# A Mamba and attention hybrid in float32: the residual added by TensorE in the turn to tokens, the last product with C by halves, z projected later in the period, and half tiles two apart

## The chip, the core and the metric

The kernel runs on one core of a Trainium2 chip. The metric is the device time of one launch in microseconds. The engines are named as in the profile: PE is TensorE (matrix multiplications; PEld its weight loads), DVE is VectorE, ACT is ScalarE, POOL is GpSimd, and SP is SyncE, which here issues most of the DMAs. Each engine works through its own queue in program order, and waits at an instruction whose inputs or whose buffer are not ready.

## What is computed

The input x has 8 batches of 128 channels and 64 x 64 pixels, so 4096 positions in each batch. There are two layers.

The first is a Mamba block over the positions, with a group norm and a residual:

```python
xz = x @ W_in;  xh, z = split(xz)                # 256 channels each
xh = silu(causal_conv_k2(xh)); x_dbl = xh @ W_x  # dt_low, B, C
dt = softplus(dt_low @ W_dt + b_dt)
h = exp(dt * A) * h + dt * B * xh;  y = sum_n h * C   # scan over positions, 16 states
y = (y + xh * D) * silu(z);  out = y @ W_out
x = silu(group_norm(out)) + x                    # the residual
```

The second layer turns x into tokens t and adds a causal additive attention (scores from tanh of a sum of two projections, summed over 16 units; weights exp(scores) below the diagonal), and then a mixture of 64 experts with the top 8 tokens for each expert. The kernel computes the sums of tanh as ratios of exponentials, D (denominators) and N (numerators), each a matrix product of vectors U and V.

## The kernel before, in words

The launch has a fast path and a general path behind a flag; only the fast path runs here. It has three stages.

**Mamba** (function `mamba`, L255 to L588). The positions are cut into 64 chunks of 512 (8 for each batch). A written-out loop, L530 to L588, runs "periods". In each period every chunk in flight is taken one step further: chunk c1 is projected, c2 gets its step sizes, c3 is scanned, c4 is gated and projected back, c5 is normalised, c6 gets its residual and c7 is turned to tokens in the same period, c8 is layer-normed, c9 gets the vectors U and V, c10 is saved to DRAM. From c5 on a chunk lies a batch (8 chunks) behind, since the group norm needs the whole batch. The order of the calls in the loop is the order of each engine's queue. 64 chunks and the lag make 79 periods: the first ones have no late steps, the last ones no early ones.

Only three of the 16 states are scanned (NR = 3); the others are summed by `over` and `others`, and `vanish` collects a number that shows whether that is allowed. Steps that matter here, with their lines:

- `project` (L283), `gate` (L294) and `silus` (L302 to L304): the projections of x and z on PE, then silu on ACT.
- `rows` (L311 to L324): B, C and the low-rank step; ACT copies bc (L315), GpSimd writes it to DRAM (L317), SP reads it back over all partitions as rep (L319), DVE forms prod (L324), which frees the PSUM buffer that the second `steps` matmul needs.
- `steps` (L330), `magnitudes` (L340 to L343), `logarithm` (L347), `rounded` (L351) and `inputs` (L356 to L360): softplus, spread over ACT and DVE.
- `decays` (L383, ACT, into two PSUM buffers of tag da), `drive` (L387, DVE), `scan` (L396, DVE) and `outputs` (L402, GpSimd: state times C), three times each, one for each state.
- `others` (L369, DVE), which reads the PSUM tile of `over` (L364, PE).
- `sums` (L408 and L410 on PE, L412 on DVE): the states' products are added by matmuls with the identity. `gated` (L416), `back` (L421), `store` (L430 on ACT, L431 on DVE).
- `normal` (L444, ACT), `residual` (L448, GpSimd), `turn` (L455, PE transposes; L457, ACT's copy to tt).
- `moments` (L461 to L471), `tokens` (L478), `turn_back` (L487 to L490), `vectors` (L498 to L502), `save` (L505).

PSUM is shared by tags: "s" has two buffers in turn (for pbc, both pdt, both py, pt, pb and po), and "pz" has one, for over, pz and puv. On SBUF, "db" is a ring of three (three drives and w in each period), tt and uv have one buffer each.

**Attention** (function `attend`, from L591). A tile is one block of 128 keys (jb) against 512 queries (ic). Above the diagonal blocks of a row a tile is narrower. The list `tiles` has for each row ic its full tiles, then a tile of two pieces (384 and 128 columns, so 512 in all), and last a half tile of 256 columns. There are 136 tiles for each batch, 1088 in all. Round i of the main loop (L1066 to L1090) works on several tiles at once:

```python
rounds(cur, nxt)        # PE: N of tile i and D of tile i + 2
inverses(i, nxt, last)  # ACT: ln of D (L650, L651), exp (L653, or L656 and L659)
causal(i - 2); ratios(cur); scores(cur)   # DVE L664, L665, L673, L678; GpSimd L666
weigh(i - 3)            # PE: weights times tokens (L687), into av
```

D and N of one round are three matrix products each, on row groups of 32, 32 and 64 rows of the array (L631). `weigh` starts the sum av at the tile with jb = 0, and ends it at the half tile, after which DVE copies it (L696). Between these steps the round takes a few items of the lanes `finishing` and `routing`, which hold the work at the end of a row and the choice of the experts' tokens. `bring` (L741 to L746) loads U, V, tt and tok of a chunk by SP, U and V in six pieces each.

**Experts** (from L1091): loads of weights, the small products, and the result.

## Time and profile before

| | |
|---|---|
| three runs, median (lowest to highest) | 6251.23 us (6249.23 to 6251.68) |
| profiled execution, its own time | 6249.68 us |
| its span, from first to last instruction | 6248.0 us |
| mean granted PE clock | 0.955 |
| busy PE, DVE, ACT, POOL | 93%, 78%, 80%, 32% of the span |
| DMA | 426.65 MB, 68 GB/s in the mean |

A row of the timeline has its start in us from the span's start, its length in us, the engine, the line, the operation with output<-inputs, the count where neighbours are merged, and in brackets the idle time of the engine before it and what released it. A row of a group has the count, then busy us and mean ns of one, then idle us before it. The granted clock is a share of full speed. Durations of matmuls are modelled and overlap; their starts give the pitch.

### The profile page before, as it was taken

The page shows a single profiled execution, that of the slowest core. Times are in us where ns is not written, and L with a number is a line of the kernel's source. Part 1 is how long each engine was busy: PE and PEld are TensorE (multiplying, and loading weights), DVE is VectorE, ACT ScalarE, POOL GpSimd, SP SyncE. Part 2 cuts the span into 40 slices and gives each one's busy share as a digit, 9 for nine tenths or more (in the row PEclk, how much of TensorE's full clock was granted, in tenths as well). Part 3 has the DMA queues.
Part 4 walks back from the last instruction along what each step waited for, and adds up shares of the span by engine and source line. Part 5 has one row for each costly group of instructions (what it writes and reads, how often), then busy time and mean ns, then how long its engine had stood idle before and what let it go on. Part 6 is the DMA issues. An engine that isn't in the chain of part 4 may idle for free. (4 is left out here: it accounts for less than half of the span.)

```text
span 6248.0 us, 69479 instructions
## 1 busy us (share of the span) xinstructions
PE 5802.7 (93%) x22714; PEld 2254.2 (36%) x22714; DVE 4860.9 (78%) x7829; ACT 4986.9 (80%) x5657; POOL 1992.1 (32%) x1652
## 2 busy tenths in 40 slices
PE   7888888888869999999999999999999999999987
PEld 2333333333323334333333333433333333343335
DVE  7999999999937777777777777777777777777741
ACT  5677777777658998898899889889889988988941
POOL 2333333333313332333333233233333323323311
PEclk8999999999879999999999999999999999999988
DMA  2234333333340011010101101101010110110058
GB/s 82 75 123 132 128 132 132 132 126 128 115 150 26 24 33 34 24 44 27 31 13 46 33 24 33 34 24 44 26 33 13 46 33 24 33 35 24 15 206 294
DMA packets 182406, 426.65 MB, mean 68 GB/s; under 512 B 32578, under 2 KB 33234, under 8 KB 171282
## 3 DMA queue, kind: packets, MB, share of 16 engines
q1 hardware_dynamic: 172514, 403.48, 19.9%
q0 software_dynamic: 9376, 18.37, 0.8%
q8 instruction: 182, 2.98, 0.2%
q14 instruction: 190, 1.56, 0.1%
q10 hardware_dynamic: 144, 0.26, 0.0%
HBM read 295.12 MB, written 126.88 MB: 68 GB/s over the span
## 5 line engine op out<-in xcount | busy, mean ns | idle before, releaser
L631 PE MATMUL D<-U,V 32*128 32x512 f32 (+7 forms) x6912 | 2730.8, 607 | 16.6 <-DMA U<-uv_dram 13.3
L631 PE MATMUL N<-U,V 32*128 32x512 f32 (+7 forms) x6912 | 2366.0, 608 | 46.6 <-DVE mix L664 44.3
L666 POOL TENSOR_TENSOR mix<-mix 128x512 f32<-128x512 f32 (+1 forms) x1088 | 1348.1, 1239 | 2833.7 <-DVE mix L664 2713.5
L653 ACT ACTIVATE mix<-mix 128x2048 f32<-128x2048 f32 x973 | 1853.2, 1905 | 31.0
L678 DVE TENSOR_TENSOR mix<-mix,mix 128x512 f32<-128x512 f32 (+1 forms) x1088 | 736.4, 677 | 920.1 <-POOL mix L666 919.9
L650 ACT ACTIVATE mix<-D 128x1024 f32<-128x1024 f32 (+1 forms) x1088 | 1077.3, 990 | 442.1 <-PE N L631 398.7
L631 PEld LDWEIGHTS D<-U,V 32*128 32x128 f32 (+1 forms) x6912 | 886.2, 185 | 1425.6 <-issue 533.8
L664 DVE TENSOR_TENSOR mix<-mix,N 128x1024 f32<-128x1024 f32 (+1 forms) x1088 | 1284.9, 1181 | 31.6 <-PE N L631 24.6
L687 PE MATMUL av<-mix,tok 128*128 128x512 f32 (+3 forms) x2304 | 1209.0, 611 | 30.0 <-DVE sums L696 28.8
L631 PEld LDWEIGHTS N<-U,V 32*128 32x128 f32 (+1 forms) x6912 | 710.8, 185 | 267.1 <-DVE mix L664 230.4
L665 DVE TENSOR_TENSOR mix<-mix,N 128x512 f32<-128x512 f32 (+1 forms) x1088 | 722.6, 664 | 1.8 <-PE N L631 1.8
L651 ACT ACTIVATE mix<-D 128x512 f32<-128x512 f32 (+1 forms) x1088 | 632.4, 581 | 17.7 <-PE N L631 15.3
L687 PEld LDWEIGHTS av<-mix,tok 128*128 128x128 f32 x2304 | 350.5, 189 | 802.2 <-issue 692.6
L402 POOL TENSOR_TENSOR hc<-hs,rep 128x1024 f32<-128x1024 f32 x192 | 453.0, 2369 | 472.3 <-issue 369.6
L396 DVE TENSOR_TENSOR_SCAN hs<-da,hs,db 128x512 f32<-128x512 f32 x336 | 412.3, 1269 | 10.8 <-ACT da L383 4.1
L410 PE MATMUL py<-hc,ident 128*128 128x512 f32 x768 | 354.1, 597 | 0.0
L383 ACT ACTIVATE da<-dt,aneg 128x512 f32<-128x512 f32 x384 | 259.2, 688 | 62.8 <-DVE hs L396 50.7
L283 PE MATMUL px<-xt,wtap 128*128 128x512 f32 x512 | 288.2, 692 | 3.9 <-DMA xt<-in_x_dram 3.9
L317 POOL DMA_DIRECT2D bc_dram<-bc x128 | 68.8, 542 | 520.5 <-ACT bc L315 520.3
L387 DVE TENSOR_TENSOR db<-dx,rep 128x1024 f32<-128x1024 f32 x192 | 228.0, 1215 | 0.1
L410 PEld LDWEIGHTS py<-hc,ident 128*128 128x128 f32 x768 | 149.7, 195 | 193.7 <-issue 193.4
L487 PE MATMUL pb<-ident,tok 128*128 128x128 f32 x256 | 74.3, 386 | 153.4 <-DVE tok L478 153.4
(243 smaller groups left out, 5659.0 us busy)
## 6 DMA issues: line engine op xcount, KB each, us to landing
rep<-bc_dram SPq DMA_DIRECT2D x64, 1536.0 KB, 7.0
uv_dram<-uv SPq DMA_DIRECT2D x64, 768.0 KB, 3.5
xr<-in_x_dram SPq DMA_DIRECT2D x64, 256.0 KB, 3.3
k_dram<-tt SPq DMA_DIRECT2D x64, 256.0 KB, 7.3
k_dram<-tok SPq DMA_DIRECT2D x64, 256.0 KB, 7.5
U<-uv_dram SPq DMA_DIRECT2D x128, 128.0 KB, 2.9
V<-uv_dram SPq DMA_DIRECT2D x128, 128.0 KB, 2.9
U<-uv_dram SPq DMA_DIRECT2D x256, 64.0 KB, 2.0
```

The costliest lines, as they stand in the source:

```text
L396: nc.vector.tensor_tensor_scan(hs[:, h, :], ch[c].pop(("da", n, h)), db[:, h, :], first, ALU.mult, ALU.add)
L402: nc.gpsimd.tensor_tensor(hc, ch[c]["hs", n], ch[c]["rep"][:, 1, n, :].unsqueeze(1).to_broadcast([P, 2, CH]), ALU.mult)
L410: nc.tensor.matmul(py, lhsT=ident, rhs=ch[c]["hc", n][:, h, :], start=False, stop=n == NR - 1)
L631: nc.tensor.matmul(t12[:, g - 1, at : at + n] if g else t0[:, at : at + n], lhsT=V[b, jb // NQ][r, ab, ts(jb % NQ, P)], rhs=U[b, ic][r, ab ...
L650: nc.scalar.activation(x[:, 1:3, lo:], d12[:, :, lo:], AF.Ln)
L651: nc.scalar.activation(x[:, 0, lo:], d0[:, lo:], AF.Ln)
L653: nc.scalar.activation(x[:, :, lo:], x[:, :, lo:], AF.Exp, scale=-1.0)
L664: nc.vector.tensor_tensor(r[:, 1:3, lo:], r[:, 1:3, lo:], n12[:, :, lo:], ALU.mult)
L665: nc.vector.tensor_tensor(r[:, 0, lo:], r[:, 0, lo:], n0[:, lo:], ALU.mult)
L666: nc.gpsimd.tensor_tensor(mix[k + 1][:, 3, lo:], r[:, 1, lo:], r[:, 2, lo:], ALU.add)
L678: nc.vector.tensor_tensor(s, s, mix[k - 2][:, 0, lo:], ALU.add)
L687: nc.tensor.matmul(av[0][:, q : q + n], lhsT=tok[b, jb // NQ][:, jb % NQ, :], rhs=mix[k + 1][:, 3, at : at + n], start=first, stop=last,)
```

## The change

In the Mamba periods the GpSimd addition of the residual is gone. `turn` adds it on PE instead: for each of four blocks a matmul of o with the identity and one of xr with the identity go into the same PSUM block. The copy to tt is a step of its own (`taken`), at the place where `turn` was; `turn` itself comes earlier, right after `gated`. The last of the three products with C is issued as two halves. `others` moves from before the scans to after the sums. `silus` is split: x first, then `gate`'s z, whose silu comes after `normal`. The tile of `vanish` is taken from the ring db, tt has two buffers, and the uv of every other chunk of the last batch takes a buffer of rep.

In attention the half tile comes first in the odd rows, and before the tile of two pieces in the even rows, so that the half tiles of two neighbouring rows stand two places apart in the list; the tile of two pieces now ends the row. `weigh` takes the first two tiles of an odd row in exchanged order, both in one round, and none in the next. `bring` loads the rows of the small groups first, and for the first chunk of all it issues U by ACT and V by GpSimd.

```diff
@@ -295,11 +295,13 @@
                     pz[:, h, :], lhsT=wgate[:, ts(h, P)], rhs=ch[c]["x"][:, 1:], start=True, stop=True
                 )
-        def silus(c):
+        def silu_x(c):
             xc = ch[c]["xc"] = pair("xc", f"xc{c}", 4)
             px = ch[c].pop("px")
             for h in range(2):
                 nc.scalar.activation(xc[:, h, :], px[:, h, :], AF.Silu, bias=convb[:, h : h + 1])
+        def silu_z(c):
             zs = ch[c]["zs"] = pair("zs", f"zs{c}", 4)
             nc.scalar.activation(zs, ch[c].pop("pz"), AF.Silu)
@@ -371,10 +373,10 @@
             )
         def vanish(c):
+            z = pair("db", f"fade{c}", 3)
             for h in range(2):
-                z = mw.tile([P, CH], F32, tag="fade", bufs=1, name=f"fade{c}_{h}")
                 nc.scalar.activation(
-                    z, ch[c]["dt"][:, h, :], AF.Exp, scale=fade[:, h : h + 1], accum_out=faded[:, c, h : h + 1]
+                    z[:, h, :], ch[c]["dt"][:, h, :], AF.Exp, scale=fade[:, h : h + 1], accum_out=faded[:, c, h : h + 1]
                 )
         def decays(c, n):
@@ -399,9 +401,12 @@
         def outputs(c, n):
             hc = ch[c]["hc", n] = pair("hc", f"hc{c}_{n}", 5)
-            nc.gpsimd.tensor_tensor(
-                hc, ch[c]["hs", n], ch[c]["rep"][:, 1, n, :].unsqueeze(1).to_broadcast([P, 2, CH]), ALU.mult
-            )
+            for h in ((slice(0, 2),) if n < NR - 1 else (slice(0, 1), slice(1, 2))):
+                hs = ch[c]["hs", n][:, h, :]
+                nc.gpsimd.tensor_tensor(
+                    hc[:, h, :], hs, ch[c]["rep"][:, 1, n, :].unsqueeze(1).to_broadcast(list(hs.shape)), ALU.mult
+                )
         def sums(c, h):
             py = single(f"py{c}_{h}")
@@ -443,18 +448,18 @@
             b, o = c // NCH, ch[c]["o"]
             nc.scalar.activation(o, o, AF.Silu, bias=norm[:, b, 1:2], scale=norm[:, b, 0:1])
-        def residual(c):
-            o = ch[c]["o"]
-            nc.gpsimd.tensor_tensor(o, o, ch[c].pop("xr"), ALU.add)
         def turn(c):
-            o = ch[c].pop("o")
+            o, xr = ch[c].pop("o"), ch[c].pop("xr")
             pt = single(f"pt{c}").rearrange("p (q c) -> p q c", c=P)
             for q in range(NQ):
-                nc.tensor.transpose(pt[:, q, :], o[:, ts(q, P)], ident)
-            t = ch[c]["t"] = mw.tile([P, NQ, P], F32, tag="tt", bufs=1, name=f"tt{c}")
-            nc.scalar.copy(t, pt)
+                nc.tensor.matmul(pt[:, q, :], lhsT=o[:, ts(q, P)], rhs=ident, start=True, stop=False)
+                nc.tensor.matmul(pt[:, q, :], lhsT=xr[:, ts(q, P)], rhs=ident, start=False, stop=True)
+            ch[c]["pt"] = pt
+        def taken(c):
+            t = ch[c]["t"] = mw.tile([P, NQ, P], F32, tag="tt", bufs=2, name=f"tt{c}")
+            nc.scalar.copy(t, ch[c].pop("pt"))
         def moments(c):
             t = ch[c]["t"]
@@ -496,7 +501,12 @@
             puv = psum.tile([P, 2, CH], F32, tag="pz", name=f"puv{c}")
             for s in range(2):
                 nc.tensor.matmul(puv[:, s, :], lhsT=wuv[:, s, :], rhs=xT, start=True, stop=True)
-            uv = ch[c]["uv"] = mw.tile([P, 3, CH], F32, tag="uv", bufs=1, name=f"uv{c}")
+            if c < NC - NCH or c % 2:
+                uv = mw.tile([P, 3, CH], F32, tag="uv", bufs=1, name=f"uv{c}")
+            else:
+                uv = mw.tile([P, 2, NR, CH], F32, tag="rep", bufs=2, name=f"uv{c}")[:, 0]
+            ch[c]["uv"] = uv
             nc.scalar.activation(uv[:, 0, :], puv[:, 0, :], AF.Exp, bias=shift)
             nc.scalar.activation(uv[:, 1, :], puv[:, 1, :], AF.Exp, bias=biasv)
             nc.scalar.activation(uv[:, 2, :], uv[:, 1, :], AF.Copy, scale=wcol)
@@ -529,9 +539,9 @@
         nc.scalar.preload_act_table_set(LOG_EXP)
         for p in range(NC + NCH + 7):
-            c1, c2, c3, c4, c5, c6, c7, c8, c9, c10 = (
+            c1, c2, c3, c4, c5, c7, c8, c9, c10 = (
                 p - i if 0 <= p - i < NC else None
-                for i in (0, 1, 2, 3, NCH + 3, NCH + 4, NCH + 4, NCH + 5, NCH + 6, NCH + 7)
+                for i in (0, 1, 2, 3, NCH + 3, NCH + 4, NCH + 5, NCH + 6, NCH + 7)
             )
             def on(c, step, *args):
@@ -552,11 +562,9 @@
             on(c3, over)
             on(c2, steps)
             on(c2, magnitudes)
-            on(c3, others)
             on(c1, project, 1)
             on(c3, scan, 0)
             on(c3, outputs, 0)
-            on(c6, residual)
             on(c3, decays, 1)
             on(c2, logarithm)
             on(c3, scan, 1)
@@ -566,21 +574,24 @@
             on(c3, scan, 2)
             on(c3, outputs, 2)
             on(c4, sums, 1)
+            on(c3, others)
             on(c3, vanish)
             on(c2, rounded)
             on(c8, tokens)
             on(c4, gated)
+            on(c7, turn)
+            on(c1, silu_x)
             on(c1, gate)
-            on(c1, silus)
             if p < NC + 3:
                 on(c5, normal)
             elif p == NC + 3:
                 for c in range(NC - NCH, NC):
                     normal(c)
+            on(c1, silu_z)
             if p <= NC + 3:
                 nc.scalar.preload_act_table_set(LOG_EXP)
-            on(c7, turn)
+            on(c7, taken)
             on(c8, turn_back)
             on(c9, vectors)
             on(c4, back)
@@ -597,13 +608,15 @@
         tiles = []
         for b in range(B):
             for ic in range(NCH):
                 d = NQ * ic
-                tiles += [(b, ic, [(jb, 0, CH, 0)]) for jb in range(d + 1)]
-                tiles.append((b, ic, [(d + 1, P, 3 * P, P), (d + 3, 3 * P, P, 0)]))
-                tiles.append((b, ic, [(d + 2, 2 * P, 2 * P, 2 * P)]))
+                row = [[(jb, 0, CH, 0)] for jb in range(d + 1)]
+                row.insert(0 if ic % 2 else d + 1, [(d + 2, 2 * P, 2 * P, 2 * P)])
+                row.append([(d + 1, P, 3 * P, P), (d + 3, 3 * P, P, 0)])
+                tiles += [(b, ic, pieces) for pieces in row]
         per = len(tiles) // B
         U, V, tok, tt, lnf = {}, {}, {}, {}, {}
         den, num, av, mix, sums, m = {}, {}, {}, {}, {}, {}
@@ -680,7 +693,7 @@
         def weigh(k):
             b, ic, pieces = tiles[k]
-            first, last = pieces[0][0] == 0, pieces[0][0] == NQ * ic + 2
+            first, last = pieces[0][0] == 0, len(pieces) == 2
             if first:
                 av[0] = ap.tile([P, CH], F32, tag="av", name=f"av{k}")
             for jb, q, n, at in pieces:
@@ -689,7 +702,7 @@
                     lhsT=tok[b, jb // NQ][:, jb % NQ, :],
                     rhs=mix[k + 1][:, 3, at : at + n],
                     start=first,
-                    stop=last,
+                    stop=last and jb == pieces[-1][0],
                 )
             if last:
                 sums[b, ic] = aw.tile([P, CH], F32, tag="sums", name=f"sums{k}")
@@ -735,11 +748,12 @@
             c = b * NCH + g
             u = U[b, g] = aw.tile([P, 2, CH], F32, tag="U", bufs=4, name=f"U{n}")
             v = V[b, g] = aw.tile([P, 2, CH], F32, tag="V", bufs=NCH + 1, name=f"V{n}")
-            for ab, to, at, k in ((0, 0, 0, 64), (1, 0, 64, 32), (1, 64, 96, 32)):
+            queues = (nc.scalar, nc.gpsimd) if c == 0 else (nc.sync, nc.sync)
+            for ab, to, at, k in ((1, 0, 64, 32), (1, 64, 96, 32), (0, 0, 0, 64)):
                 for which in range(2):
                     rows = slice(to + k * which, to + k * (which + 1))
-                    nc.sync.dma_start(u[rows, ab, :], uv_dram[c][0, at : at + k, :])
-                    nc.sync.dma_start(v[rows, ab, :], uv_dram[c][1 + which, at : at + k, :])
+                    queues[0].dma_start(u[rows, ab, :], uv_dram[c][0, at : at + k, :])
+                    queues[1].dma_start(v[rows, ab, :], uv_dram[c][1 + which, at : at + k, :])
             t = tt[b, g] = aw.tile([P, NQ, P], F32, tag="tt", bufs=6, name=f"tt{n}")
             k = tok[b, g] = aw.tile([P, NQ, P], F32, tag="tok", bufs=NCH + 1, name=f"tok{n}")
             for r, dst in enumerate((t, k)):
@@ -1063,6 +1077,7 @@
             bring(0, g)
         lanes = [finishing, routing]
         n = len(tiles)
+        weighed = []
         for i in range(-2, n + 3):
             cur = i if 0 <= i < n else None
             nxt = i + 2 if i + 2 < n else None
@@ -1085,8 +1100,12 @@
             if cur is not None:
                 ratios(cur)
                 scores(cur)
-            if i >= 3:
-                weigh(i - 3)
+            if i >= 3 and i - 3 not in weighed:
+                order = [i - 3] if off(i - 3) == 0 or tiles[i - 4][:2] == tiles[i - 3][:2] else [i - 2, i - 3]
+                for k in order:
+                    weigh(k)
+                weighed = order
             advance("p", 1)
         wb1 = aw.tile([NE, NH * P], F32, tag="wb1", name="wb1")
         nc.sync.dma_start(wb1, weight1[:, P, :])
```

## The prediction

> **What bounds the kernel now.** I read, in this order, the busy time by stage, the costliest groups with shapes kept apart, and the timeline, engine by engine: periods of the Mamba stage, its end, and rounds of attention. The stages first (columns: start:end, length, busy time and instructions of PE, PEld, DVE, ACT and POOL, then granted clock, DMA share, GB/s):
>
> ```profile
> 310.00:1690.00 1380.00, 1202.76 (x2842) 503.26 (x2841) 1330.89 (x1797) 1020.42 (x1627) 492.89 (x365) 0.92 0.39 129
> 1690.00:1816.00 126.00, 74.68 (x176) 33.54 (x174) 45.34 (x171) 61.83 (x112) 22.75 (x26) 0.71 0.42 148
> 1816.00:5950.00 4134.00, 4049.57 (x17541) 1482.95 (x17544) 3136.69 (x5364) 3641.57 (x3547) 1334.75 (x1078) 0.99 0.10 31
> 5950.00:6248.00 298.00, 235.14 (x1666) 138.72 (x1658) 92.57 (x227) 72.33 (x92) 44.78 (x77) 0.85 0.73 262
> ```
>
> Two thirds of the time is attention, where TensorE is busy 98%. In the Mamba periods (first row) it is VectorE, 96% (1330.9 of 1380), with TensorE at 87% and a granted clock of 0.92. The change removes no VectorE instruction, so I asked what holds VectorE there. The groups:
>
> ```profile
> L402 POOL TENSOR_TENSOR hc<-hs,rep 128x1024 f32<-128x1024 f32 x192 | 453.0, 2369 | 472.3 <-issue 369.6 <-DVE hs L396 87.4 <-PE py L410 7.7
> ...
> L351 DVE TENSOR_SCALAR w<-u 128x1024 f32<-128x1024 f32 x64 | 154.1, 2407 | 4.1 <-ACT u L343 4.1
> ```
>
> L351 is a tensor_scalar on 1024 elements, 2407 ns in the mean, though its first two, with GpSimd idle, took 0.69 and 0.72 us. One period of the timeline shows why:
>
> ```profile
> 829.45 1.26 POOL L448 TENSOR_TENSOR o<-o,xr 128x512 f32<-128x512 f32 x1
> 830.68 4.65 POOL L402 TENSOR_TENSOR hc<-hs,rep 128x1024 f32<-128x1024 f32 x2
> ...
> 833.02 2.87 DVE L351 TENSOR_SCALAR w<-u 128x1024 f32<-128x1024 f32 x1
> ...
> 836.20 1.24 PE L487 MATMUL pb<-ident,tok 128*128 128x128 f32 x4 [2.99 <-DVE tok L478]
> 837.23 2.86 PE L498 MATMUL puv<-xT,wuv 128*128 128x512 f32 x4
> ```
>
> GpSimd runs the residual (1.26), then two products back to back, until 830.68 + 4.65 = 835.33. VectorE's L351 starts at 833.02 and ends at 835.89, 0.56 after GpSimd lets go; a period earlier the two ends are 809.50 and 810.05. So L351 waits for GpSimd: its successor starts 2.79 us after it, alone that would be 0.65, the wait is 2.14. TensorE meanwhile stands 2.99 us for the tokens, and then runs cold: puv takes 2.86 where four such matmuls take 1.88.
>
> Attention's 1088 rounds, timed between starts of the L650 logarithm, take 3.82 us in the mean, 3.87 where all tiles near are full, 3.27 where VectorE has little else to do. D and N run side by side in different rows of the array, so a half D beside a full N saves TensorE nothing: here the 256 columns of D are through, and the 512 of N still run.
>
> ```profile
> 2406.04 0.38 PE L631 MATMUL D<-U,V 64*128 64x256 f32 x1
> ...
> 2406.26 0.59 PE L631 MATMUL N<-U,V 64*128 64x512 f32 x1
> ```
>
> **The change, part by part.** The sum is made against the profiled execution, 6249.68 us (its span 6248.0 and 1.7 around it); the median of the three runs, 6251.23, is 1.5 more.
>
> *Residual and halves.* GpSimd loses 1.26 us per period. Its last product becomes two of 128x512; L448, that shape, took 1279 ns, so 2.5 for both against 2.37, but the first can begin when half of the scan is done. I walk the new queues from the end of L324 (P = 846.46 in this period), with the pitches of the trace. VectorE: moments and last drive to P + 2.50; then, `others` (1.13) having moved behind the sums, the first scans to 4.98. GpSimd: first product 4.98 to 7.35, second to 10.5, the halves to 11.75 and 13.0. VectorE, with the stand below, comes to L351 at 12.85 and waits 0.15. Gain 2.0 of a 25.56 us period; if `others` did not stand ahead of L351, 1.1 of that would be waited for again.
>
> *What is late next.* The second pair of decays. ScalarE's chain begins when VectorE has the moments (L470, P + 1.37); four activations and an exponential follow, and the first decay starts at P + 4.95 and is ready at 5.64. Today VectorE wants it at about 6.1, now at 4.98, and stands about 0.72. That leaves 25.56 - 2.14 + 0.15 + 0.72 = 24.3.
>
> *Turn by TensorE.* Four transposes (0.45) become eight matmuls, sixteen instructions, each with its weight load. The nearest row is L757, whose four 128x129 instructions take 0.61, a pitch of 0.11: 16 x 0.11 = 1.8 us, +1.3; at half clock 3.5. TensorE's walk: second pdt at P + 0.1, px to 3.0, sums to 10.1, turn to 11.9, gate 12.9 to 14.65, pb 15.1, puv 15.75 to 17.5, po 19.2, pbc 20.9, px 22.6, over and the first pdt 23.6. The 2.99 us hole covers the turn: nothing on the path. Without that cover it would be 1.3 x 51 = 66 us.
>
> *z later, `others` later.* over, gate and puv share one PSUM buffer, so gate now waits for `others` (12.85); behind it on TensorE are pb, puv and po, and behind the silu of z on ScalarE a table load, both copies, three uv activations and the copy of o, for which VectorE's L431 waits. From the end of `others`: gate 1.75, silu 1.05, load 1.3, copies 0.96, uv 1.95, o 0.55, in all 7.6; VectorE gets to L431 7.7 after it. So 0, with 0.1 to spare. The fade tile, now in the db ring, waits for a scan that ended 3 us before: 0.
>
> *Clock.* Here rule and row differ.
>
> ```profile
> 374.39 1.52 PE L330 MATMUL pdt<-bc,wdt 8*128 8x512 f32 x2 [1.36 <-DVE prod L324]
> 375.84 3.78 PE L283 MATMUL px<-xt,wtap 128*128 128x512 f32 x4
> ```
>
> The Trainium skill (TensorE: Matmul & The Clock Gate, "HAM oscillation — how this bites in real kernels") has the clock fall when an idle gap passes a window of some 3.4 us. In these rows a wait of 1.36, after matmuls of 8 and 16 rows, is followed by px at 3.78, half speed. By the rule the new order, with gaps of 1.0, 0.65 and 0.6, is never cold, and the period is 24.3. By the row px and the first sum can be cold still and 1.7 late, of which 1.0 is slack at y: up to 0.7 more, 25.0. I take the row in a third of the periods: 24.5.
>
> From 366 to 1679 us there are 44 ordinary periods, 25.8 in the mean: 1.3 each, 57. Those that close a batch and their followers I leave at 0 (L351 took 1.05 there already). In 11 periods of the filling, where L351 took 2.18 and no moments hold ScalarE, 1.4 each: 15. Mamba periods: -72 (bounds: -26 at 25.2, -116 at 23.5).
>
> *The end of Mamba,* some 9 periods of 7.3 us:
>
> ```profile
> 1781.10 0.59 ACT L457 COPY tt<-pt 128x512 f32<-128x512 f32 x1 [3.98 <-DMA k_dram<-tt]
> ...
> 1785.96 2.95 PE L498 MATMUL puv<-xT,wuv 128*128 128x512 f32 x4
> ```
>
> The tile's second buffer takes away the 3.98 us wait for its store (the uv tiles in two places only keep the next such wait from coming). Next in the loop: rs 0.45, tok and pb 0.9 + 1.2, puv 3.0, uv 2.0, some 7.5 cold, no gain; warm 0.45 + 0.5 + 0.5 + 1.7 + 2.0 = 5.2. With the sixteen instructions TensorE is busy 4.0 of 5.2, so warm for most of it: between 0 and -19 I take 1.7 x 9 = -15. The first loads of attention leave SP, where twelve issues took some 0.5 each, for ScalarE and GpSimd, both idle then (12.8 and 33 us); the first rows go out first and land about 2.0 later, near 1818.5, where the first matmul started at 1821.09. V through GpSimd's queue no row shows; a slower one would give the gain back: -3 to 0, I take -3.
>
> *Half tiles two apart.* The 64 halves meet in 32 rounds in which both D and N are half. Such a round needs TensorE 1.06 + 1.06 instead of 3.18, ScalarE 2.05 instead of 3.22, VectorE 1.5: 2.3 to 2.6. For the two rounds with one half each today (3.76 and 3.88 in the mean) there is one of 2.5 and a full one, 3.87: a gain of 1.3 at most. As the chain of logarithms stands behind it, and VectorE's finishing work falls in the same rounds, I take 0.7: 32 x 0.7 = -22 (bounds 0 and -42). Two tiles weighed in one round at a row's start are one fewer in the next: 0.
>
> Sum: 6249.7 - 72 - 15 - 3 - 22 = 6137.7; +1.5 to the median: **6139**.
>
> **The rivals.**
> *Attention and the end of Mamba give nothing* (logarithms hold the pair's round, the last periods stay cold): 6251 - 75 = 6176. For it: a half today saves only some 0.7 over the six rounds around it. Against: in the pair's round every engine's work is halved at once. Chance 0.20.
> *TensorE becomes the period's bound, with nothing lost.* Its work is 22.0 us at full clock (23.6 in the walk less 1.6 of waits); at 0.853 that is 25.8, today's period, and only the other parts stay: 6251 - 40 = 6211. Chance 0.12.
> *Slower: the same, below that clock.* Its place is the Mamba period; it decides from 0.853 down; at 0.80 the period is 27.5, and 1.7 x 51 = 87 less 40 gives 6298. For it: the clock is only 0.92 there now, and small matmuls are added. Against: the hole ahead of the cold puv is filled. Chance 0.07.
> *Better than the sum:* decays in time and no window cold (-116), the last loop warm (-19), loads -3, the pair in full (-42): 6071. Chance 0.10.
> *As summed:* 0.51, within 6110 to 6165.
>
> **Numbers.** A measurement can tell about 0.2%, 12.5 us, from no change. The range 6085 to 6205 leaves out the slower case, about half of the one at 6211 and half of the best: 0.18. Faster 0.90 (all but the slower case and a quarter of the one at 6211), same 0.03, slower 0.07.
>
> **What would show it.** L351 at about 0.7 us in nearly every period; ordinary periods near 24.5; a stand of some 0.7 for the second decays; no wait for the tokens on TensorE, and a clock above 0.95 in the stage; no wait of the tt copy for its store; 32 rounds of about 2.5. I am wrong if L351 still ends half a microsecond after GpSimd, if the copy of o comes after VectorE is at L431, if px and the sums run cold in most periods, or if a pair's round takes over 3.3.

## The result and the profile after

| | before | after |
|---|---|---|
| runs beside each other, median (lowest to highest) | 6250.23 us, four (6246.75 to 6251.68) | 6152.54 us, four (6145.28 to 6157.12) |
| ratio to before, 95% interval | | 0.9843 (0.9826 to 0.9860) |
| profiled execution, its span | 6249.68, 6248.0 us | 6154.11, 6152.3 us |
| mean granted PE clock | 0.955 | 0.972 |

The changed kernel is 1.6% faster, 98 us. The forecast was 6139 us, 13.5 below the median, a gain of 112 where 98 came; the time lies inside the range. In the changed file the lines are a few further down: `rounded` is L353 (was L351), `scan` L398 (L396), `outputs` L407 (L402), `others` L371 (L369), `store`'s statistics L436 (L431), `tokens` L483 (L478), the copy to tt L462 (L457), `vectors` L503 (L498), the rounds' matmuls L644 (L631), their logarithm L663 (L650), `bring` L755 and L756 (L741 and L742).

First the busy time by stage, in the columns of the first view of before:

```profile
310.00:1610.00 1300.00, 1193.44 (x3438) 537.02 (x3437) 1221.51 (x1775) 998.73 (x1616) 435.46 (x364) 0.98 0.40 135
1610.00:1730.00 120.00, 85.55 (x325) 51.92 (x323) 51.91 (x188) 65.85 (x120) 8.45 (x16) 0.85 0.47 168
1730.00:5860.00 4130.00, 4016.07 (x17586) 1480.70 (x17586) 3140.05 (x5373) 3651.93 (x3572) 1343.82 (x1087) 0.99 0.10 31
5860.00:6152.00 292.00, 227.64 (x1623) 136.04 (x1616) 86.19 (x216) 63.41 (x82) 41.40 (x74) 0.84 0.74 267
```

The clock of the Mamba periods went from 0.92 to 0.98. The groups that carried the argument:

```profile
L407 POOL TENSOR_TENSOR hc<-hs,rep 128x1024 f32<-128x1024 f32 x128 | 302.4, 2363 | 414.2 <-issue 294.8 <-DVE hs L398 115.9 <-PE py L413 2.3
L407 POOL TENSOR_TENSOR hc<-hs,rep 128x512 f32<-128x512 f32 x128 | 160.8, 1278 | 8.7 <-DVE hs L398 8.7
...
L353 DVE TENSOR_SCALAR w<-u 128x1024 f32<-128x1024 f32 x64 | 55.6, 868 | 4.1 <-ACT u L345 4.1
```

L353 takes 868 ns where it took 2407. One period of the timeline, VectorE, GpSimd and TensorE in turn:

```profile
820.51 2.46 DVE L398 TENSOR_TENSOR_SCAN hs<-da,hs,db 128x512 f32<-128x512 f32 x2 [0.79 <-ACT da L385]
...
827.53 0.96 DVE L353 TENSOR_SCALAR w<-u 128x1024 f32<-128x1024 f32 x1
```

```profile
819.86 2.36 POOL L407 TENSOR_TENSOR hc<-hs,rep 128x1024 f32<-128x1024 f32 x1 [5.63 <-issue]
823.11 4.83 POOL L407 TENSOR_TENSOR hc<-hs,rep 128x1024 f32<-128x1024 f32 x3 [0.90 <-DVE hs L398]
```

```profile
826.32 0.39 PE L457 MATMUL pt<-ident,xr 128*128 128x128 f32 x2
827.77 1.96 PE L294 MATMUL pz<-xt,wgate 128*128 128x512 f32 x4 [1.06 <-DVE y L371]
...
830.84 1.98 PE L503 MATMUL puv<-xT,wuv 128*128 128x512 f32 x4 [0.68 <-ACT zs L306]
```

GpSimd ends at 823.11 + 4.83 = 827.94, and L353 at 828.49, still 0.55 after it; but now it starts only 0.41 before GpSimd ends. The new stand of VectorE is there too: 0.79 us for the second decay. Before, it went through both pairs of scans without a stop:

```profile
824.53 5.04 DVE L396 TENSOR_TENSOR_SCAN hs<-da,hs,db 128x512 f32<-128x512 f32 x4
```

TensorE now waits 1.06 for `others` and 0.68 for zs, and puv runs at full speed (1.98, was 2.86).

Where the time went, from starts of VectorE's and ScalarE's instructions in the two profiled executions (the `inputs` of the 14th and of the last chunk, and attention's first and last logarithm; the first row counts from the span's start):

| stretch | before | after | difference | predicted |
|---|---|---|---|---|
| start and filling | 365.8 | 356.5 | -9.3 | -15 |
| 50 steady periods | 1313.3 | 1251.8 | -61.5 | -57 |
| last period to attention's first logarithm | 145.9 | 130.5 | -15.4 | -18 |
| attention, 1088 rounds | 4150.0 | 4135.9 | -14.0 | -22 |
| after the last logarithm | 273.0 | 277.6 | +4.6 | 0 |

The sum is -95.6. Ordinary periods went from 25.80 to 24.59 in the mean and from 25.58 to 24.44 in the median.

### The profile page after: what moved, and what is told of

Its sections match the earlier page's. It is cut to its first block, busy times and chain, and to the rows that moved or that the text cites. A ratio compares the mean times of both kernels' runs of the same rounds, so it can differ in the third digit from the quotient of the medians.

```text
span 6152.3 us, 71062 instructions
## 1 busy us (share of the span) xinstructions
PE 5768.0 (94%) x23482; PEld 2303.7 (37%) x23482; DVE 4747.3 (77%) x7829; ACT 4973.3 (81%) x5672; POOL 1928.0 (31%) x1658
## 5 line engine op out<-in xcount | busy, mean ns | idle before, releaser
L644 PE MATMUL D<-U,V 32*128 32x512 f32 (+7 forms) x6912 | 2716.4, 606 | 16.7 <-DMA V<-uv_dram 12.6
L644 PE MATMUL N<-U,V 32*128 32x512 f32 (+7 forms) x6912 | 2362.6, 606 | 50.8 <-DVE mix L677 49.0
L679 POOL TENSOR_TENSOR mix<-mix 128x512 f32<-128x512 f32 x1088 | 1350.4, 1241 | 2798.2 <-DVE mix L677 2767.9
L666 ACT ACTIVATE mix<-mix 128x2048 f32<-128x2048 f32 x958 | 1831.8, 1912 | 30.6
L691 DVE TENSOR_TENSOR mix<-mix,mix 128x512 f32<-128x512 f32 x1088 | 736.4, 677 | 923.1 <-POOL mix L679 923.0
L663 ACT ACTIVATE mix<-D 128x1024 f32<-128x1024 f32 x1088 | 1076.9, 990 | 431.8 <-PE N L644 406.9
L644 PEld LDWEIGHTS D<-U,V 32*128 32x128 f32 (+1 forms) x6912 | 877.7, 185 | 1410.9 <-issue 490.0
L677 DVE TENSOR_TENSOR mix<-mix,N 128x1024 f32<-128x1024 f32 x1088 | 1285.1, 1181 | 28.4 <-PE N L644 28.0
L644 PEld LDWEIGHTS N<-U,V 32*128 32x128 f32 (+1 forms) x6912 | 713.8, 184 | 275.3 <-DVE mix L677 235.2
L678 DVE TENSOR_TENSOR mix<-mix,N 128x512 f32<-128x512 f32 x1088 | 723.3, 665 | 0.8 <-PE N L644 0.8
L664 ACT ACTIVATE mix<-D 128x512 f32<-128x512 f32 x1088 | 632.0, 581 | 15.2 <-PE N L644 14.2
L407 POOL TENSOR_TENSOR hc<-hs,rep 128x1024 f32<-128x1024 f32 (+1 forms) x256 | 460.6, 1820 | 422.9 <-issue 294.8
L398 DVE TENSOR_TENSOR_SCAN hs<-da,hs,db 128x512 f32<-128x512 f32 x336 | 412.6, 1270 | 51.8 <-ACT da L385 49.5
L294 PE MATMUL pz<-xt,wgate 128*128 128x512 f32 x256 | 131.2, 636 | 67.1 <-DVE y L371 67.1
```

The source lines that it names most:

```text
L398: nc.vector.tensor_tensor_scan(hs[:, h, :], ch[c].pop(("da", n, h)), db[:, h, :], first, ALU.mult, ALU.add)
L407: nc.gpsimd.tensor_tensor(hc[:, h, :], hs, ch[c]["rep"][:, 1, n, :].unsqueeze(1).to_broadcast(list(hs.shape)), ALU.mult)
L644: nc.tensor.matmul(t12[:, g - 1, at : at + n] if g else t0[:, at : at + n], lhsT=V[b, jb // NQ][r, ab, ts(jb % NQ, P)], rhs=U[b, ic][r, ab ...
L663: nc.scalar.activation(x[:, 1:3, lo:], d12[:, :, lo:], AF.Ln)
L664: nc.scalar.activation(x[:, 0, lo:], d0[:, lo:], AF.Ln)
L666: nc.scalar.activation(x[:, :, lo:], x[:, :, lo:], AF.Exp, scale=-1.0)
```

## The experiments

Theory 1 is the prediction's: VectorE sets the period, and it gained because GpSimd lets L353 go earlier, less the new stand for the decay. Its rival, theory 2: the gain came from TensorE, whose hole the turn fills and whose clock the longer work keeps up. All twelve kernels were timed beside the kernel before; the ratio in the table is to it. Where two of these kernels are compared below, it is by the last column, since they were timed at different times; the tables of periods and the waits come from one profiled execution each.

| run | median us | ratio (95% interval) | against before, us |
|---|---|---|---|
| after | 6152.54 | 0.9843 (0.9826 to 0.9860) | -98 |
| e1_attention_only | 6234.39 | 0.9980 (0.9973 to 0.9987) | -13 |
| e2_mamba_only | 6159.30 | 0.9863 (0.9848 to 0.9878) | -88 |
| e3_residual_gpsimd | 6191.80 | 0.9910 (0.9894 to 0.9925) | -56 |
| e4_unsplit | 6168.23 | 0.9871 (0.9856 to 0.9886) | -79 |
| e5_others_early | 6162.22 | 0.9872 (0.9857 to 0.9887) | -83 |
| e6_decays_first | 6117.88 | 0.9795 (0.9781 to 0.9808) | -127 |
| e8_tt_one | 6164.69 | 0.9870 (0.9854 to 0.9885) | -84 |
| e9_no_residual | 6201.51 | 0.9925 (0.9911 to 0.9939) | -44 |
| e10_gpsimd_sixteen | 6159.40 | 0.9865 (0.9850 to 0.9880) | -86 |
| e11_decays_bring | 6105.97 | 0.9775 (0.9761 to 0.9788) | -143 |
| e12_pair_free | 6145.70 | 0.9838 (0.9824 to 0.9851) | -103 |
| e13_best | 6100.97 | 0.9767 (0.9754 to 0.9781) | -146 |

**The two parts alone.** The first kernel is the one before with the new list of tiles and `weigh`; the second is the changed one with the old list and weighing, so it keeps the new `bring`. The second's edit, in part:

```diff
-                row = [[(jb, 0, CH, 0)] for jb in range(d + 1)]
-                row.insert(0 if ic % 2 else d + 1, [(d + 2, 2 * P, 2 * P, 2 * P)])
-                row.append([(d + 1, P, 3 * P, P), (d + 3, 3 * P, P, 0)])
-                tiles += [(b, ic, pieces) for pieces in row]
+                tiles += [(b, ic, [(jb, 0, CH, 0)]) for jb in range(d + 1)]
+                tiles.append((b, ic, [(d + 1, P, 3 * P, P), (d + 3, 3 * P, P, 0)]))
+                tiles.append((b, ic, [(d + 2, 2 * P, 2 * P, 2 * P)]))
```

> The kernel before with only the attention part of the change: the half tiles two apart and the weighing that goes with it. If the parts add up, this is what the two profiles give for attention (4149.96 to 4135.91 us, -14.0) and its tail (+4.6): -9, so about 6241 us (6234 to 6246). By the prediction's own term it would be -22: 6229. By the view that the halves gain nothing where VectorE carries the finishing work: only the first pair of each batch gains, 8 x 2.5 = -20 in attention, and the other 24 pairs give 6 of it back. If the Mamba part had changed attention (through the place of its last transfers or the clock), this run would differ from -9 by more than 4.

> The changed kernel with the tile order and the weighing of before: the Mamba part and the queues of the first loads alone. If the parts add up: -97.7 + 9 = -88, so about 6162 us (6156 to 6168), with ordinary periods of 24.4 to 24.6 us as in the whole change. If half of the Mamba gain hung on something that attention shares, it would be above 6180.

Measured -13 and -88, together -101 where the whole gave -98: the parts add up within the intervals. Ordinary periods of the second took 24.59, as in the whole.

**The residual back on GpSimd**, with four transposes in the turn:

```diff
+            nc.gpsimd.tensor_tensor(o, o, ch[c].pop("xr"), ALU.add)
...
-                nc.tensor.matmul(pt[:, q, :], lhsT=o[:, ts(q, P)], rhs=ident, start=True, stop=False)
-                nc.tensor.matmul(pt[:, q, :], lhsT=xr[:, ts(q, P)], rhs=ident, start=False, stop=True)
+                nc.tensor.transpose(pt[:, q, :], o[:, ts(q, P)], ident)
```

> The changed kernel with the residual back on GpSimd behind the first product, and the turn by four transposes; everything else as changed. Theory 1 (the gain is L353's wait for GpSimd that ended): GpSimd stands idle 0.90 us between its first and second product, so 0.9 of the residual's 1.28 is covered; its chain ends 0.4 later and L353 with it: a period of 24.8, +0.4 x 51 = +20 us, about 6173. Theory 2 (the gain is that the turn's sixteen instructions fill TensorE's hole and keep its clock up): TensorE has 1.3 us less to do in the hole, px is cold again, the granted clock of the stage falls from 0.98 to 0.93 and the period goes to 25.2 or more: +40 to +60, 6193 to 6213.

It lost 42 us against the changed kernel, which is theory 2's number, and the granted clock from 310 to 1600 us is 0.93 where it was 0.98. L353 took 1.13 where it took 0.90 (steady periods), only 0.23 more. TensorE, VectorE and ScalarE in one period of its timeline:

```profile
814.39 0.60 PE L460 MATMUL pt<-ident,o 128*128 128x128 f32 x4
817.39 3.64 PE L294 MATMUL pz<-xt,wgate 128*128 128x512 f32 x4 [2.41 <-DVE y L371]
```

```profile
821.08 1.02 ACT L306 ACTIVATE zs<-pz 128x1024 f32<-128x1024 f32 x1 [3.05 <-PE pz L294]
```

```profile
826.91 0.69 DVE L436 BATCH_NORM_STATS2 gst<-o 128x6 f32<-128x512 f32 x1 [1.43 <-ACT o L435]
```

The turn is short, so TensorE waits 2.41 for `others` instead of 1.06; the gate that follows runs at 3.64 instead of 1.96. Everything behind it on ScalarE comes that much later, and VectorE stands 1.43 at L436 for the copy of o. This is the chain in which the prediction had "0.1 to spare".

Two more kernels part the two effects: one has no residual at all, so the turn is four transposes of o; the other has the residual on GpSimd and keeps TensorE at sixteen instructions, with four of the eight matmuls on a matrix of zeros. Their diffs in `turn`:

```diff
-                nc.tensor.matmul(pt[:, q, :], lhsT=o[:, ts(q, P)], rhs=ident, start=True, stop=False)
-                nc.tensor.matmul(pt[:, q, :], lhsT=xr[:, ts(q, P)], rhs=ident, start=False, stop=True)
+                nc.tensor.transpose(pt[:, q, :], o[:, ts(q, P)], ident)
```

```diff
-                nc.tensor.matmul(pt[:, q, :], lhsT=xr[:, ts(q, P)], rhs=ident, start=False, stop=True)
+                nc.tensor.matmul(pt[:, q, :], lhsT=xr[:, ts(q, P)], rhs=nought, start=False, stop=True)
```

> The changed kernel with the residual left out altogether: the turn is four transposes of o alone and xr is loaded but not used, so TensorE has 1.3 us less to do in each period and GpSimd nothing more. Theory A (the sixteen instructions are worth something of their own: they fill TensorE's wait for others before the gate, and without them the gate starts after a wait of 2.4 and runs at half speed, 0.85 to 0.91 a matmul where it was 0.61, and the copy of o comes late at L436): as in the run with the residual on GpSimd less what GpSimd made of it (L353 1.13 against 0.90, 0.24): 24.44 + 0.6 = 25.05, +31 us over the changed kernel, about 6181. Theory B (all of that run's loss came from GpSimd): 24.4 or a little less, 6145 to 6152.

> The changed kernel with the residual on GpSimd behind the first product, and TensorE still at sixteen instructions in the turn (its second four multiply xr by a matrix of zeros). Theory A: the gate is warm, no stand at L436, and only GpSimd's 0.24 to 0.4 is lost at L353: 24.7 to 24.8, +12 to +20, 6162 to 6170. Theory B: as the run with the residual on GpSimd and four transposes, +42: 6192.

| ordinary period, mean us | sixteen instructions on TensorE | four transposes |
|---|---|---|
| no residual on GpSimd | 24.59 (after) | 25.42 (e9) |
| residual on GpSimd | 24.74 (e10) | 25.47 (e3) |

The kernel that leaves the residual out loses 54 us to the one that does it on TensorE. From 310 to 1600 us, the waits of e9:

```profile
PE pz L294 <- DVE y L371: 110.2, 50, 2.5
...
DVE gst L436 <- ACT o L435: 50.3, 47, 1.7
```

and of after:

```profile
PE pz L294 <- DVE y L371: 43.4, 51, 1.3
...
DVE gst L436 <- ACT o L435: 4.6, 11, 1.6
```

VectorE's stand at L436 is 50.3 us in 50 periods against 4.6 in 51: 0.9 a period, about the 0.83 that the period grew. With sixteen instructions the stand is 5.7 us in e10. So in the new order the longer turn is worth 0.73 to 0.83 a period, and freeing GpSimd of the residual 0.05 to 0.15 (profiles with the same Mamba code differ by up to 0.05, 24.54 to 24.59).

What the longer turn does is shown, but not quite which property of it. The two turns differ in kind as well as in length: four transposes against sixteen instructions of plain matmuls. A short turn of plain matmuls was not run. For the length speaks that a wait of 2.16 behind the sixteen plain ones is followed by slow matmuls too; the rows stand with the end of Mamba below.

Is the longer turn then where the gain comes from? No: before the change VectorE hardly stood at this place (310 to 1690 us):

```profile
DVE gst L431 <- ACT o L430: 7.3, 20, 1.1
```

There was nothing there to win. The new order made the wait ahead of the gate, and the longer turn keeps it harmless. Nor is it GpSimd's loss of the residual by itself: with the residual on GpSimd and the turn long (e10), 1.06 of the 1.21 us that the ordinary period gained are still there. GpSimd stands idle for 0.90 between its first and second product, so most of the residual fits in. The halves, the residual and the place of `others` cover for each other, and no run has the old order with one of them alone; how the 1.21 divides among them stays open.

**The product in one piece, and `others` early.** First the product:

```diff
-            for h in ((slice(0, 2),) if n < NR - 1 else (slice(0, 1), slice(1, 2))):
+            for h in (slice(0, 2),):
```

> The changed kernel with the last product on GpSimd in one piece again. Theory 1: the halves start at 825.5 when the second product ends; one piece waits for the second half of the scan, 825.9, and ends 0.35 later, L353 with it: +0.35 x 51 = +18, about 6170 us; L353 takes 1.2 instead of 0.87. Theory 2 (TensorE's hole): 6152, no change. If both scan halves finish before GpSimd is free, the split is worth nothing and L353 gets shorter by 0.1 (one piece is 2.37, two halves 2.5): 6147.

Measured +18.6 against the changed kernel; L353 1.29 where it took 0.90, ordinary periods 24.98, both +0.39: theory 1's numbers. A later end of GpSimd goes into the period in full, so VectorE, with L353's wait, is on the path. Next, `others` back in its old place:

```diff
+            on(c3, others)
             on(c1, project, 1)
             on(c3, scan, 0)
...
             on(c4, sums, 1)
-            on(c3, others)
```

> The changed kernel with others (VectorE, 1.22 us) back ahead of the first scan. VectorE has the same work. By the walk: the scans begin 1.13 later, the stand of 0.79 for the second decay is absorbed, so GpSimd's end comes 0.34 later against VectorE's start of the period; L353, with nothing between it and the last sum, starts 1.1 earlier against that and ends 0.55 after GpSimd as now: it takes 2.3 instead of 0.90 and the period grows by 0.34 to 24.8; +0.34 x 51 = +17, about 6167. The gate, which waits for others, would then be free of its wait of 1.06 and the silu of z of its 1.36. If it is that wait on TensorE that holds the period, this run is faster than the changed kernel: 23.9, 6125.

It gained 14.6 less than the changed kernel, near the 17 that I expected, but not for the reason I gave. Ordinary periods took 24.55, as in the changed kernel; the six that close a batch took 29.6 where they took 28.1 to 28.7, which makes 8. The profiled execution was at the low end of its runs (6154), so what the rest is can't be read from it. L353 took 1.13, not 2.3. VectorE and GpSimd in its timeline show what became of the wait:

```profile
802.17 0.84 DVE L353 TENSOR_SCALAR w<-u 128x1024 f32<-128x1024 f32 x1
802.93 2.06 DVE L483 TENSOR_SCALAR tok<-tt,lmv,rs 128x128 f32<-128x128 f32 x4
```

```profile
798.87 5.27 POOL L407 TENSOR_TENSOR hc<-hs,rep 128x1024 f32<-128x1024 f32 x3 [0.24 <-DVE hs L398]
```

L353 slips in and ends at 803.01, while GpSimd works until 804.14; the next tensor_scalar, L483, now takes 2.06 for four where it took 1.10. The two waits are 0.19 (0.84 - 0.65) and 0.96, together 1.15: the 1.1 that the prediction said `others` covers. The stand for the decay (43.2 us in the stage) fell to 2.9 in return, so the period stayed.

**The decays first.** ScalarE's exponential of u goes behind the second pair of decays and the logarithm behind the third:

```diff
-            nc.scalar.activation(u, u, AF.Exp, scale=-1.0)
...
             on(c3, decays, 1)
-            on(c2, logarithm)
+            on(c2, exponential)
...
             on(c3, decays, 2)
+            on(c2, logarithm)
```

> The changed kernel with ScalarE's exponential of u behind the second pair of decays and the logarithm behind the third, so that the second pair starts 1.07 us earlier. If VectorE's stand of 0.79 us for the second decay is what the new period still loses, as the prediction has it: the scans, GpSimd's products, others and the gate all come 0.79 earlier, the stand vanishes from the waits, the ordinary period goes from 24.44 to 23.65, and the time by 0.79 x 51 = 40, to about 6110 us. If TensorE (22.0 us of work and waits for others and for zs of 1.06 and 0.68) or ScalarE's chain behind zs becomes late instead, only a part: 24.0, about 6130. If the stand was cover for GpSimd, so that L353 waits 0.8 more: no change, 6150.

It gained 30 us on the changed kernel. Ordinary periods took 23.87 in the mean, 0.72 less. VectorE now goes through both pairs of scans without a stop:

```profile
802.56 5.05 DVE L401 TENSOR_TENSOR_SCAN hs<-da,hs,db 128x512 f32<-128x512 f32 x4
```

So the stand was on the path, and nearly its whole length came out: 0.72 of 0.79.

**The end of Mamba and the first loads.**

```diff
-            t = ch[c]["t"] = mw.tile([P, NQ, P], F32, tag="tt", bufs=2, name=f"tt{c}")
+            t = ch[c]["t"] = mw.tile([P, NQ, P], F32, tag="tt", bufs=1, name=f"tt{c}")
```

> The changed kernel with one buffer for the turned tile (tt) in the Mamba stage, as before the change; the rest as changed. If the second buffer is what shortens the end of Mamba: the copy at the last periods waits again some 4 us for its store, the loop of a drain period goes from 5.7 to 7.3 us and 9 of them make +14; the gap from the last ordinary period to attention's first logarithm is 145 where it was 126 to 130. If the warm TensorE (sixteen instructions) carries most of it: 6.3 a period, +5. Ordinary periods: the same, as the store of 256 KB is long done when the next copy comes, 24 us later. Total about 6163.

Measured +13.5 against the changed kernel; the gap to attention was 143.0. ScalarE's copy waits for its store again, and the loop is 7.3 long (from 1700.95 to 1708.26):

```profile
1700.95 0.58 ACT L462 COPY tt<-pt 128x512 f32<-128x512 f32 x1 [4.31 <-DMA k_dram<-tt]
...
1708.26 0.58 ACT L462 COPY tt<-pt 128x512 f32<-128x512 f32 x1 [3.98 <-DMA k_dram<-tt]
```

TensorE ran at full speed in most of these periods all the same (puv 1.88), so its clock by itself gains nothing here; without the second buffer the loop is as long as before the change. That the second buffer alone is the cause doesn't follow. In the changed kernel one of these periods had a slow puv:

```profile
1670.79 0.39 PE L457 MATMUL pt<-ident,xr 128*128 128x128 f32 x2
1673.33 1.25 PE L492 MATMUL pb<-ident,tok 128*128 128x128 f32 x4 [2.16 <-DVE tok L483]
1674.37 3.40 PE L503 MATMUL puv<-xT,wuv 128*128 128x512 f32 x4
...
1681.59 1.88 PE L503 MATMUL puv<-xT,wuv 128*128 128x512 f32 x4
...
1687.34 1.88 PE L503 MATMUL puv<-xT,wuv 128*128 128x512 f32 x4
```

From the slow puv to the next it is 7.2, from there on 5.7; the kernel with the decays first has one such period, of 7.1. So, as far as these two show it, the gain needs both, the second buffer and the full clock, as the prediction had it (7.5 cold, 5.2 warm). The buffer with a slow TensorE throughout was not run.

The next kernel has the decays first and one more edit, in `bring`; the small groups still go first:

```diff
-            queues = (nc.scalar, nc.gpsimd) if c == 0 else (nc.sync, nc.sync)
+            queues = (nc.sync, nc.sync)
```

> The changed kernel with two edits: the exponential and the logarithm behind the decays (as in the run with that alone, 0.9795 of before) and the first loads of attention all on SP's queue again, in the new order (small groups first). If the split over ScalarE and GpSimd is a loss, as the profile of after has it (last save to first D 10.6 us against 8.9 before; V waited 15.5 on GpSimd's queue for the ones of tok): last save to first D at 6.9 to 8.9, -2 to -4 us, 6114. If SP's twelve issues in a row are slower than that: 11 to 13, 6119.

It gained 15 us more than the decays alone (142.9 and 127.5, each beside its own runs of before). The last save and the first matmul of attention, in before, in after and in this kernel:

```profile
1812.20 0.37 SPq L505 DMA_DIRECT2D uv_dram<-uv  x1
...
1821.09 2.87 PE L631 MATMUL D<-U,V 32*128 32x512 f32 x3 [13.29 <-DMA U<-uv_dram]
```

```profile
1724.49 0.37 SPq L515 DMA_DIRECT2D uv_dram<-uv  x1
...
1728.52 4.48 ACTq L755 DMA_DIRECT2D U<-uv_dram  x6
...
1731.97 3.10 POOL L756 DMA_DIRECT2D V<-uv_dram  x6 [15.54 <-DMA tok<-k_dram]
...
1735.05 5.64 PE L644 MATMUL D<-U,V 32*128 32x512 f32 x6 [12.64 <-DMA V<-uv_dram]
```

```profile
1684.90 0.37 SPq L518 DMA_DIRECT2D uv_dram<-uv  x1
...
1688.58 0.32 SPq L759 DMA_DIRECT2D U<-uv_dram  x1
1688.95 0.42 SPq L760 DMA_DIRECT2D V<-uv_dram  x1
...
1691.35 3.47 PE L648 MATMUL D<-U,V 32*128 32x512 f32 x4 [8.54 <-DMA U<-uv_dram]
```

From the save to the first D: 8.9 before, 10.6 after, 6.45 with SP's queue and the new order. So the order of the rows was worth 2.4 and the split over two queues cost 4.1 (3.8 against the kernel with the decays alone, where it was 10.3): GpSimd issued V only 7.5 us after the save. The other 11 of the 15 us are no more than the two comparisons are uncertain by (each by some 8 either way).

**Attention's pairs.** VectorE's items of the lanes are left out of the round with two halves and of the one before it:

```diff
-            advance("v", 3)
+            pairs = [k for k in (i, i + 1) if 0 <= k < n - 2 and off(k) and off(k + 2)]
+            if not pairs:
+                advance("v", 3)
```

> The changed kernel with VectorE's finishing and routing items (advance "v") left out of the round in which both D and N are half tiles and of the round before it; they come in the rounds after. Theory A (the pair's round gains nothing in row pairs 2/3 to 6/7 because such an item stands ahead of ratios in it or in the round before, and holds N's bank): the 24 pairs of these rows gain up to 1.3 us each, as the first pair of each batch does: attention -15 to -30 us, about 6122 to 6137; row pairs of 116.4, 163.0 and 204.4 us would become 115, 162 and 203. Theory B (VectorE is the bound over the row as a whole there, the sum of items counts and not their place): the items cost in other rounds what they save here, within 5 us of the changed kernel. Worse than the changed kernel (over 6157) if routing finishes late and the last rows' items move into the tail.

Measured 5.5 less than the changed kernel, which is not clear of noise. By pairs of rows, from the starts of the logarithms (mean of the second to the seventh batch, us):

| rows | before | after | e12 |
|---|---|---|---|
| 0, 1 | 39.0 | 36.2 | 36.1 |
| 2, 3 | 115.7 | 116.4 | 113.9 |
| 4, 5 | 162.6 | 163.0 | 164.8 |
| 6, 7 | 205.0 | 205.0 | 204.9 |

The pair's round, from the logarithm of a half tile to the next, in rows 4 and 5 of after and then of e12:

```profile
3502.93 0.60 ACT L663 ACTIVATE mix<-D 128x512 f32<-128x512 f32 x1 [0.38 <-PE N L644]
...
3507.11 1.02 ACT L663 ACTIVATE mix<-D 128x1024 f32<-128x1024 f32 x1 [1.78 <-PE N L644]
```

```profile
3495.42 0.58 ACT L663 ACTIVATE mix<-D 128x512 f32<-128x512 f32 x1
...
3497.99 1.02 ACT L663 ACTIVATE mix<-D 128x1024 f32<-128x1024 f32 x1
```

In after it takes 4.2, with such an item in it; in 14 of the 16 pairs of rows 2 to 5 it takes 4.0 to 4.2. In e12 it takes 2.6 in all of them. But the other rounds, which got the items, grew: rows 2 and 3 are 2.5 shorter in all, rows 4 and 5 are 1.8 longer. That is nearer to theory B. In rows 6 and 7 nothing changed; the round is short there already. The logarithms of after show it:

```profile
4203.44 1.02 ACT L663 ACTIVATE mix<-D 128x1024 f32<-128x1024 f32 x1
...
4206.88 0.58 ACT L663 ACTIVATE mix<-D 128x512 f32<-128x512 f32 x1
...
4209.45 1.02 ACT L663 ACTIVATE mix<-D 128x1024 f32<-128x1024 f32 x1 [0.32 <-PE N L644]
...
4212.77 1.00 ACT L663 ACTIVATE mix<-D 128x1024 f32<-128x1024 f32 x1
```

The pair's round is 4209.45 - 4206.88 = 2.57 long, as forecast, but a full one there is 3.3, not 3.87. And it replaces nothing long: in these rows two rounds are clearly shorter than 3.3, of 2.4 and 2.6 in the mean; before, with the halves apart, there were two as well, of 2.5 and 2.3.

**All that gained, together**, and in the very last row the half tile at the end:

```diff
+                if (b, ic) == (B - 1, NCH - 1):
+                    row.append(row.pop(0))
```

> Everything that gained, together: decays ahead of the exponential and the logarithm, the first loads on SP's queue in the new order (these two gave 0.9775 of before), VectorE's items out of the pair's round and the one before it (row pair 2/3 shorter by 2.5 us, row pair 4/5 longer by 1.8: -5), and in the last row of the last batch the half tile at the end instead of the start, so that the last round is a short one. The tail after the last logarithm was 273.1 before and 272.1 with the old order of tiles; with the new order it was 272.9 to 281.2 in nine profiles. If the longer last round is the cause, -4: tail 272 to 273, in all 6106 - 5 - 4 = 6097 us. If the tail's length only scatters (loads of the last stage that come at other times), it stays at 277 and the time at 6101.

6100.97, ratio 0.9767: 0.8% below the changed kernel, and not to be told from the kernel with decays and loads alone (0.9775). The tail was 276.9 us although its last round was short, so the longer last round is not what lengthened it. What did stays open.

## Why the prediction was right, and where it was not

- **L353's wait.** Right: 2.14 went to some 0.25. It still ends 0.55 after GpSimd, which I had named as a sign of being wrong. The sign was badly chosen: what counts is how long before that end L353 comes up, and that is 0.41 now. The walk of the queues gave 24.3 for an undisturbed period; 24.44 is the median. Right too was what `others` covers (1.15 measured, 1.1 said), though I had not seen that the next tensor_scalar can take the wait over.
- **What is late next.** Right: 0.79 for the second decay against 0.72, shown to be on the path by taking it away. Wrong for the filling: I wrote that no moments hold ScalarE there, but VectorE stood 12.2 us for decays in 6 waits between 95 and 340 us, against 2.2 before. The -15 came out as -9.3.
- **The turn by TensorE, "nothing on the path".** The sum was right and its reason was not. I had the hole cover the turn, and priced the turn without cover at +66 us. In fact the turn covers the hole: with the short turn in it, the gate waits longer, runs cold, and the copy of o is late. The spare 0.1 in that chain was correct, so I should have asked what a shorter turn would do. I also made the 1.26 us that GpSimd loses the first item of the gain; it is worth 0.05 to 0.15 in the new order.
- **Clock.** The row was the better guide. I put a third of the periods at a cold px; between 600 and 1500 us, 9 of 36 periods have it (over 2.5 us for four matmuls), and the mean lies 0.15 over the median. The Trainium skill (TensorE: Matmul & The Clock Gate, "HAM oscillation — how this bites in real kernels") gives the rule that TensorE should have no idle gap over some 3.4 us. By it the gate after a wait of 2.41 would be warm and e9 no slower than after; in e9, 31 of the 35 gates in that stretch took 2.6 to 3.6, all after waits of 2.14 to 2.41, and the other four 1.96, after waits of 1.57. The measurement decides: a gap below that length can be followed by slow matmuls.
- **Batch-closing periods at 0.** Wrong by 8 us: the six became 1.4 shorter each, as the ordinary ones did. With 44 ordinary ones of -1.21 instead of -1.3 that is 53 + 8 = 61.5 where 57 was said.
- **End of Mamba.** The loop came out at 5.7 (5.2 warm was forecast), by the buffer and the full clock together. **First loads:** wrong in sign, +1.7 instead of -3. I had named the slower queue as a risk, and no row showed it.
- **Half tiles, -22.** The sum of -14 is within the bounds by luck, the mechanism failed. The step was "there is one of 2.5 and a full one, 3.87". 3.87 is a mean over rounds of 3.3 and rounds of up to 6.6 that carry items; where nothing else sits, a full round is 3.3. A half beside a full tile also saved more than nothing: before, rounds of 2.5 and 2.3 at the ends of rows 6 and 7. My 3.76 and 3.88 for the two rounds with one half do not come out of the trace of before: counted between logarithms they are 3.5 and 3.65 over all rows. And in 14 of the 32 pairs the pair's round took over 3.3, a sign of being wrong that I had named. The gain is 2.8 us a batch in rows 0 and 1 (8 x 2.8 = 22), and rows 2 to 5 give 1.1 back.

The rivals: "TensorE becomes the bound" and the slower case fell with the clock at 0.98. "Attention and the end of Mamba give nothing" holds for three of four row pairs. In the profiled executions the sum of -112 fell short by 16: attention 8, the filling 6, the tail 5 and the end of Mamba 3, less 5 won in the steady periods.

## What to carry to other kernels

When a move shortens one engine's wait, walk the other queues through the new order and find the chain with the least slack: here it was gate, silu of z, and the copy of o, with 0.1 us, and the work that seemed a cost of the change was what kept it in time. After a gain, look for the next stand on the bounding engine; moving two instructions on ScalarE gave another 30 us. And take the length of a round from the rounds where the edit acts, not from a mean.

## What the hardware showed that was not expected

- Doing less made it slower: without the residual, 6201.5 us against 6152.5.
- In e3 and e9, from 340 to 1590 us, the gate's four matmuls took 1.96 after waits of 1.57; after waits of 2.14 to 2.54 they took 2.4 to 3.65 in 76 of 81 cases, and 1.96 in five. In the filling of e9, where no turn stands ahead, eight waits of 2.00 left them at 1.96 five times and at 2.4 to 2.9 three times, and one of 2.58 left them at 1.96. So it is not the wait alone. To count the transposes as idle does not settle it either: with their 0.60 added the slow gates follow 2.7 to 3.1, but so do the five exceptions (2.8 to 3.1). Nor are transposes needed: at the end of Mamba four kernels (after, e6, e12, e13) have a wait of 2.1 to 2.2 behind sixteen plain instructions, and puv then took 3.15 to 3.45 where it takes 1.88. What else decides stays open.
- A tensor_scalar of 1024 elements can come in between two GpSimd instructions (0.84 us in e5, with GpSimd busy before and after), and then the next one waits.
